# A transformer stack on one core: the last attention first, then the last two pairs' GLU one after another

## The chip, the cores and the metric

The kernel runs on one core of a Trainium2 chip. The metric is device microseconds of one execution, taken as the median over several runs. A profiled execution gives the trace, in which every instruction of every engine has its start and its length. The engines are TensorE (PE in the profile, PEld for its weight loads), VectorE (DVE), ScalarE (ACT), GpSimd (POOL) and SyncE (SP), which issues the transfers.

## The reference

The input is x, 16 sequences of 256 tokens with 128 features, in float32. Two blocks with residual follow. The first is a causal attention with 16 heads of 8 on a normalized x. The second, on the normalized sum, is a stack of 6 layers, each of them an attention in windows of 32 tokens and a gated unit (GLU):

```python
for i in range(DEPTH):                                   # 6
    x = attn_layer(shift_tokens(x), Wqkv[i], ...) + x    # 16 heads of 64, windows of 32
    x = ffn_layer(shift_tokens(x), ...) + x

def ffn_layer(x, g, bln, W1, b1, W2, b2):
    xn = layernorm(x) * g + bln
    a, gate = split(xn @ W1 + b1)                        # 341 each
    return a * gelu(gate) @ W2 + b2
```

`shift_tokens` takes half of the features from the token before. No sequence needs another one, so the stack can run over sequences and layers in a staggered order.

## The kernel before, in words

A first stage does the causal attention, writes its sum to `out` in memory and leaves the normalized, transposed sum in SBUF: `yT[b]`, 128 features by 512 tokens, that is, a pair of sequences. The second stage is the stack. It counts sequences through all layers, n = 0 to 95 (layer n // 16, sequence n % 16), and pairs m = 0 to 47; pair m is sequences 2m and 2m+1, so the last pair is 47, with n = 94 and 95, and the second last is 46.

The loop at the end runs `half(n, u)` for n from -2 to 98 and u = 0, 1. A half works on several sequences at once. For sequence n it does half of the heads: `sim` (scores, 64 matmuls per call pair), `soften` (DVE: scale `sm` and maximum `mx`; POOL: subtract), `power` (ACT: exp, tile `ex`), and, one half later, `share` (DVE: sum and reciprocal; POOL or DVE: product), `attn_T` (transposes and an ACT copy, tile `aT`) and `attn_v` (tile `po`, 64 small matmuls each for x = 0 and 1, and an ACT copy to `ao` after each). `proj_v` makes the values: matmul `v`, ACT copy `vn`, and transfers on SP from `vn` to a shifted copy `vs`. `project_out` (matmul `wo`, DVE add to `yT`) comes another half later. For later sequences the same half does `proj_qk`, norms and `shift`. Where n reaches the end, the calls for sequences that don't exist fall away (`do`), so the last halves have less and less beside them.

The GLU of a pair of 512 columns is spread over the halves of the next sequences: `glu_shift` (POOL, tile `x2`), `glu_center` (matmul `cen`, ACT square `fsq` and copy `xc`), `glu_var` (matmuls `pv`, ACT copy `vr`), `glu_turn` (transpose `vT`, DVE `var`, POOL `rstd`), `glu_norm` (transposes `rs`, DVE `xn`, POOL scale), `glu_part` three times (matmuls `hg` and `ha`, ACT gelu `g`, DVE product `h`), `glu_out` (matmuls `w`, DVE add to `yT`). Every float32 matmul stands in the trace as two passes; a pair's `hg`, `ha` and `w` are 18 passes. In the last layer `leave(s)` follows for each sequence: transposes `fin`, a load of `out[s]` into `res`, a DVE add and the store. `x2` and `g` share one buffer (tag `gl`).

In the kernel before, pair 46 is shifted in half (94, 1), centred and turned in (95, 0), normed with parts 0 and 1 in (95, 1), part 2 in (96, 0), out and left in (96, 1). Pair 47 has its shift in (96, 1) and the rest in halves of 97 and 98, which hold nothing else.

The order on each engine: `in_order` adds to each instruction of a half a dependency on the one before it on the same engine, for halves with 0 <= n < 96. So up to half (95, 1) the order on the engines is as written; after that a scheduler places the instructions.

Of the kernel before, what the change touches and what calls it, by code (L numbers as in the profile page):

```python
# [7 lines left out]
F32 = mybir.dt.float32  # L8
# [3 lines left out]
ALU = mybir.AluOpType  # L12
# [3 lines left out]
NSEQ, S, E = 16, 256, 128  # L16
# [17 lines left out]
V_G, V_B, V_B2, V_B1, V_QK = 0, 1, 2, 3, 9  # L34
# [4 lines left out]
def tile_transformer(  # L39
# [16 lines left out]
    nc = tc.nc  # L56
    P = 128
# [6 lines left out]
    ident = cst[:, C_ID : C_ID + 128]  # L64
# [6 lines left out]
    vecs = const.tile([P, DEPTH, V_ALL], F32, name="vecs")  # L71
# [17 lines left out]
    def in_order(traced, pinned):  # L89

        for i in nc.cur_bb.bb.instructions[traced:]:
            if i.engine not in engines:
                continue
            if pinned and i.engine in last:
                tc.add_manual_dep(
                    i,
                    last[i.engine],
                    mybir.DependencyInfo(mybir.DependencyClass.NoSync, mybir.DependencyReason.DATA),
                    reason="in_order",
                )  # L100
            last[i.engine] = i.name


    with ExitStack() as st:
# [249 lines left out]
        for s in range(-3, NSEQ + 3):  # L354
            traced = len(nc.cur_bb.bb.instructions)
# [22 lines left out]
    with ExitStack() as st:  # L378
# [18 lines left out]
        def psum1(name):  # L397
            return ps_o.tile([P, 512], F32, tag="o", name=name)
# [63 lines left out]
        def shifted(dst, s):  # L462
            y = yT[s // 2][:, (s % 2) * S : (s % 2 + 1) * S]
            nc.gpsimd.tensor_copy(dst[0:64, :], y[0:64, :])
            nc.gpsimd.memset(dst[64:128, 0:1], 0.0)
            nc.gpsimd.tensor_copy(dst[64:128, 1:S], y[64:128, 0 : S - 1])
# [228 lines left out]
        x2s, bcs, sms = {}, {}, {}  # L695


        def glu_shift(m):
            b = m % 8
            x2 = x2s[m] = p1.tile([P, 2 * S], F32, tag="gl", name=f"x2_{m}")  # L700
            for i in range(2):
                shifted(x2[:, i * S : (i + 1) * S], 2 * b + i)

        def glu_center(m):
            x2 = x2s.pop(m)
            ps = psum1(f"cen_{m}")
            nc.tensor.matmul(ps, center, x2, start=True, stop=True)
            sq2 = p1.tile([P, 2 * S], F32, tag="h1", name=f"fsq_{m}")
            nc.scalar.activation(sq2, ps, AF.Square)
            xc = p1.tile([P, 2 * S], F32, tag="h2", name=f"xc_{m}")  # L710
            nc.scalar.copy(xc, ps)
            xns[m] = sq2, xc

        def glu_var(m):
            sq2, xc = xns[m]
            pv = psum1(f"pv_{m}")

            for t in range(4):
                nc.tensor.matmul(
                    pv[32 * t : 32 * t + 32, :P], mean32, sq2[:, t * P : (t + 1) * P], start=True, stop=True  # L720
                )
            rows = p1.tile([P, P], F32, tag="vr", name=f"vr_{m}")
            nc.scalar.copy(rows, pv[:, :P])
            xns[m] = rows, xc

        def glu_turn(m):
            rows, xc = xns[m]
            pv = psum1(f"vT_{m}")
            nc.tensor.transpose(pv[:, :P], rows, ident)
            var = p4.tile([P, 4], F32, tag="var", name=f"var_{m}")  # L730
            nc.vector.tensor_scalar(var, pv[:, :P].rearrange("p (t k) -> p t k", k=32)[:, :, 0], 1e-5, None, ALU.add)
            rstd = p4.tile([P, 4], F32, tag="rstd", name=f"rstd_{m}")
            rsqrt(rstd, var)
            xns[m] = rstd, xc

        def glu_norm(m):
            l = m // 8
            rstd, xc = xns[m]
            ps = psum1(f"rs_{m}")
            for t in range(4):  # L740
                nc.tensor.matmul(
                    ps[:, t * P : (t + 1) * P],
                    rstd[:, t : t + 1].to_broadcast([P, P]),
                    ident,
                    start=True,
                    stop=True,
                    is_transpose=True,
                )
            xn = p1.tile([P, 2 * S], F32, tag="xn", name=f"xn_{m}")
            nc.vector.tensor_tensor(xn, ps, xc, ALU.mult)  # L750
            nc.gpsimd.tensor_scalar(xn, xn, vecs[:, l, V_G : V_G + 1], vecs[:, l, V_B : V_B + 1], ALU.mult, ALU.add)
            xns[m] = xn

        def glu_part(mm, i):
            l = mm // 8
            if mm % 8 == 0 and i == 0:
                load_glu(l)
            xn = xns[mm]
            a, m = DI_PARTS[i]
            pg, ph = psum1(f"hg_{mm}_{i}"), psum1(f"ha_{mm}_{i}")  # L760
            nc.tensor.matmul(pg[:m], W["1"][:, DI + a : DI + a + m], xn, start=True, stop=True)  # L761
            nc.tensor.matmul(ph[:m], W["1"][:, a : a + m], xn, start=True, stop=True)  # L762
            g = p1.tile([P, 2 * S], F32, tag="gl", name=f"g_{mm}_{i}")
            nc.scalar.activation(g[:m], pg[:m], AF.Gelu, bias=vecs[:m, l, V_B1 + 3 + i : V_B1 + 4 + i])
            h = p1.tile([P, 2 * S], F32, tag=f"h{i}", name=f"h_{mm}_{i}")
            nc.vector.scalar_tensor_tensor(
                h[:m], ph[:m], vecs[:m, l, V_B1 + i : V_B1 + i + 1], g[:m], ALU.add, ALU.mult
            )
            hs[mm, i] = h

        def glu_out(mm):
            l, b = divmod(mm, 8)
            ps = psum1(f"w2_{mm}")
            for i, (a, m) in enumerate(DI_PARTS):
                nc.tensor.matmul(ps, W["2"][:m, i, :], hs[mm, i][:m], start=(i == 0), stop=(i == 2))  # L775
            nc.vector.scalar_tensor_tensor(yT[b], ps, vecs[:, l, V_B2 : V_B2 + 1], yT[b], ALU.add, ALU.add)

        def leave(s):

# [17 lines left out]
        def do(n, f, *a):  # L797
            if has(n):
                f(n, *a)
# [6 lines left out]
        def half(n, u):  # L806
            even = n % 2 == 0
            m = n // 2 - 1 if even else (n - 3) // 2
            glu = lambda m: 0 <= m < N // 2
            i, j = 2 * u, 2 * u + 1  # L810
            b, bu = (n, 0) if u else (n - 1, 1)
            bi, bj = 2 * bu, 2 * bu + 1
            do(b, share, bi)
            do(b, share, bj)
            do(n, sim, u, 0)
            do(n, sim, u, 1)
            for k in range(2):
                do(n + 2, proj_qk, i, k)
            if u == 0:
                do(n + 1, sums)  # L820
            else:
                do(n + 1, spread_k, 1)
                do(n + 1, norm_k, 1)
                if not even and glu(m):
                    glu_norm(m)
            do(n, sim, u, 2)
            do(n, sim, u, 3)
            do(n, soften, i)
            do(n, soften, j)
            do(n - 1, project_out, u)  # L830
            if u:
                do(n + 3, shift)
                if even and glu(m):
                    glu_shift(m)
            elif has(n + 1):
                roots(n + 1, n2s.pop(n + 1))
            do(b, attn_T, bi)
            do(b, attn_T, bj)
            do(n, proj_v, u, 0)
            do(b, attn_v, bi)  # L840
            if not even and u == 0 and glu(m):
                glu_center(m)
            do(n + 2, proj_qk, j, 0)
            if even and u == 0 and glu(m - 1):
                glu_part(m - 1, 2)
            if not even and glu(m):
                if u == 0:
                    glu_var(m)
                else:
                    glu_part(m, 0)  # L850
                    glu_part(m, 1)
            do(n + 2, proj_qk, j, 1)
            if not even and u == 0 and glu(m):
                glu_turn(m)
            if u == 0:
                do(n + 1, spread_k, 0)
                do(n + 1, norm_k, 0)
            do(n, power, i)
            do(n, power, j)
            do(b, attn_v, bj)  # L860
            do(*((n, masks, 1) if u == 0 else (n + 1, masks, 0)))
            if even and u and glu(m - 1):
                glu_out(m - 1)
                if m - 1 >= (DEPTH - 1) * 8:
                    leave(2 * ((m - 1) % 8))
                    leave(2 * ((m - 1) % 8) + 1)
            do(n, proj_v, u, 1)

        do(0, shift)
        last.clear()  # L870
        for n in range(-2, N + 3):
            for u in range(2):
                traced = len(nc.cur_bb.bb.instructions)
                half(n, u)
                in_order(traced, 0 <= n < N)

# [94 lines left out]
```

## Time and profile before

| | us |
|---|---|
| median of 3 runs | 3625.76 (3624.58 to 3628.56) |
| the profiled execution | 3618.6 |
| its span | 3616.8 |
| PE busy in the span | 3471.4 |
| DVE / POOL / ACT busy | 2832.4 / 2570.5 / 1882.4 |

The span is the time from the first to the last event of the profile; the execution's own time is 1.8 us longer. Busy time says how long an engine had an instruction in it. The chain that ended last follows the work back from the last instruction to what released it. The granted clock is that of TensorE, 1.00 for full speed.

### The profile page before, as it was taken

How to read it: one execution, taken by the hardware profiler on the slowest of the kernel's cores; microseconds unless marked ns; L12 is line 12 of the kernel's file. 1: busy time of each engine (PE TensorE's matmuls, PEld its weight loads, DVE VectorE, ACT ScalarE, POOL GpSimd, SP SyncE). 2: the span in 40 equal slices, each digit the busy share in tenths (PEclk: the TensorE clock that was granted, in tenths of full speed). 3: DMA queues.
4: the chain of work that ended last, by engine and by line, in shares of the span. 5: the costliest groups of instructions: out<-in, count | busy, mean ns of one | idle time of the engine just before them, and what ended most of it. 6: DMA issues, size and time to landing. Idle time of an engine off the chain costs nothing.

```text
span 3616.8 us, 153872 instructions
## 1 busy us (share of the span) xinstructions
PE 3471.4 (96%) x68080; PEld 2423.2 (67%) x68080; DVE 2832.4 (78%) x4866; ACT 1882.4 (52%) x3180; POOL 2570.5 (71%) x2731
## 2 busy tenths in 40 slices
PE   7999799999999999999999999999999999999998
PEld 5777466666666666666666666666666666666664
DVE  5665788887888888888887888887887888888784
ACT  2444355555555555555555555555555555555553
POOL 3221778778777778777777777777777778777772
PEclk9999899999999999999999999999999999999999
DMA  2000333334433334343334333334433343433332
GB/s 83 8 10 10 88 98 100 101 88 111 111 100 86 97 101 109 103 106 101 80 99 119 104 91 100 96 91 117 111 95 83 100 109 90 107 104 95 100 105 61
DMA packets 249445, 331.68 MB, mean 92 GB/s; under 512 B 74446, under 2 KB 105548, under 8 KB 247884
## 3 DMA queue, kind: packets, MB, share of 16 engines
q1 hardware_dynamic: 248060, 321.14, 33.9%
q8 instruction: 536, 8.78, 1.0%
q14 instruction: 129, 1.06, 0.1%
q10 hardware_dynamic: 720, 0.70, 0.1%
HBM read 28.14 MB, written 4.19 MB: 9 GB/s over the span
## 4 chain that ended last, share of the span: by engine, by line
PE 77%; DVE 9%; issue 7%; POOL 3%; ACT 2%; DMA 2%; SPq 0%; POOLq 0%; DVEq 0%; ACTq 0%
PE qk L485 18%; PE po L668 11%; PE v L568 9%; PE wo L688 8%; PE sim L605 6%; PE w L775 4%; PE hg L761 3%; PE ha L762 3%; PE aT L648 2%; PE n L506 2%; DVE tq L558 2%; PE bc L544 2%; DVE t L487 2%; PE sim L585 2%; ACT aT L650 1%
## 5 line engine op out<-in xcount | busy, mean ns | idle before, releaser
L487 DVE TENSOR_TENSOR t<-qk,ab 128x1024 f32<-128x1024 f32 x768 | 916.1, 1218 | 280.7 <-ACT sq L486 245.1
L499 POOL TENSOR_TENSOR tq<-t 128x512 f32<-128x512 f32 x768 | 961.7, 1273 | 89.8 <-DVE t L487 66.5
L485 PE MATMUL qk<-xs,wqk 128*128 128x256 f32 x3072 | 792.1, 394 | 1.6 <-DVE yT L693 1.5
L496 POOL TENSOR_TENSOR sq<-sq 128x512 f32<-128x512 f32 x384 | 489.0, 1274 | 339.0 <-ACT sq L486 329.6
L485 PEld LDWEIGHTS qk<-xs,wqk 128*128 128x128 f32 x3072 | 555.1, 191 | 156.0 <-issue 54.9
L486 ACT ACTIVATE sq<-qk 128x512 f32<-128x512 f32 x768 | 459.4, 598 | 352.5 <-PE qk L485 345.4
L650 ACT COPY aT<-aT 128x512 f32<-128x512 f32 x384 | 207.6, 586 | 599.3 <-PE aT L648 598.8
L668 PEld LDWEIGHTS po<-aT,vs 64*64 64x64 f32 x12288 | 327.4, 134 | 203.4 <-issue 108.7
L568 PE MATMUL v<-wv,xs 128*128 128x512 f32 x768 | 421.9, 631 | 27.6 <-ACT aT L650 21.2
L626 POOL TENSOR_TENSOR sm<-sm,mx 128x512 f32<-128x512 f32 x384 | 396.2, 1043 | 29.1 <-DVE mx L625 27.8
L668 PE MATMUL po<-aT,vs 64*64 64x32 f32 x12288 | 394.3, 222 | 8.7 <-issue 4.2
L605 PEld LDWEIGHTS sim<-us 64*32 64x32 f32 x24576 | 262.0, 105 | 205.8 <-issue 190.5
L668 PE MATMUL po<-aT,vn 64*64 64x32 f32 x12288 | 386.7, 219 | 4.6 <-issue 4.6
L574 ACT COPY vn<-v 128x512 f32<-128x512 f32 x384 | 225.2, 587 | 308.3 <-PE v L568 304.9
L688 PE MATMUL wo<-ao,wout 128*128 128x256 f32 x1536 | 383.2, 392 | 1.0 <-ACT ao L677 1.0
L668 PEld LDWEIGHTS po<-aT,vn 64*64 64x64 f32 x12288 | 330.0, 135 | 6.8 <-issue 6.8
L605 PE MATMUL sim<-us 64*32 64x64 f32 (+1 forms) x24576 | 324.6, 221 | 3.5 <-DMA us<-tq 2.8
L642 POOL TENSOR_TENSOR ex<-ex,rec 128x512 f32<-128x512 f32 x288 | 296.5, 1044 | 40.4 <-DVE rec L640 19.7
L688 PEld LDWEIGHTS wo<-ao,wout 128*128 128x128 f32 x1536 | 276.0, 189 | 49.5 <-ACT ao L677 1.7
L677 ACT COPY ao<-po 128x512 f32<-128x512 f32 x384 | 222.8, 580 | 119.0 <-PE po L668 118.8
L639 DVE TENSOR_REDUCE rec<-ex 128x8 f32<-128x512 f32 x384 | 251.8, 656 | 34.1 <-ACT ex L632 34.1
L625 DVE TENSOR_REDUCE mx<-sm 128x8 f32<-128x512 f32 x384 | 263.4, 686 | 13.3
(125 smaller groups left out, 5196.4 us busy)
## 6 DMA issues: line engine op xcount, KB each, us to landing
us<-tq SPq DMA_DIRECT2D x768, 256.0 KB
vs<-vn SPq DMA_DIRECT2D x384, 192.0 KB
vs<-vn SPq DMA_DIRECT2D x192, 64.0 KB
wqk<-in_f_wqkv_dram SPq DMA_DIRECT2D x96, 64.0 KB
ab<-in_tables_dram SPq DMA_DIRECT2D x6, 1024.0 KB
wv<-in_f_wqkv_dram SPq DMA_DIRECT2D x12, 256.0 KB
wout<-in_f_wo_dram SPq DMA_DIRECT2D x24, 128.0 KB
x<-in_x_dram SPq DMA_DIRECT2D x16, 128.0 KB
```

Of the source, the lines that this page charges most:

```text
L485: nc.tensor.matmul(ps[:, t * S : t * S + S], W["qk", g][:, k, t, :], xs[n], start=True, stop=True)
L486: nc.scalar.activation(sq2[:, k].rearrange("p t n -> p (t n)"), ps, AF.Square)
L487: nc.vector.tensor_tensor(t12[:, k].rearrange("p f t n -> p f (t n)"), ps.unsqueeze(1).to_broadcast([P, 2, 2 * S]), W["ab", l][:, k].rearr ...
L496: nc.gpsimd.tensor_tensor(sq[n, g], sq2[:, :, 0, :], sq2[:, :, 1, :], ALU.add)
L499: nc.gpsimd.tensor_tensor(tq[n, g][:, t], t12[:, :, 0, t, :], t12[:, :, 1, 1 - t, :], ALU.add)
L568: nc.tensor.matmul(ps, xs[n][:, P * c : P * c + P], W["v"][:, u].rearrange("p g x d -> p (g x d)"), start=True, stop=True)
L605: nc.tensor.matmul(ps[WIN * r : WIN * r + WIN, x, col + first : col + 64], qk[part, g, 0, WIN * c : WIN * c + WIN], qk[part, g, 1, WIN * ( ...
L625: nc.vector.tensor_reduce(mx, seg, AX.X, ALU.max)
L626: nc.gpsimd.tensor_tensor(seg, seg, mx.unsqueeze(2).to_broadcast([P, 8, 64]), ALU.subtract)
L642: on.tensor_tensor(seg, seg, rec.unsqueeze(2).to_broadcast([P, 8, 64]), ALU.mult)
L668: nc.tensor.matmul(po[DH * y : DH * y + DH, h, x, g, WIN * r : WIN * r + WIN], v[64 * h : 64 * h + 64, r // 2, 2 * g + y, x, :], aT[64 * h ...
L688: nc.tensor.matmul(ps[:, :S].rearrange("p (h m) -> p h m", h=2), W["out"][:, g, 2 * u + x, :], a[:, x, :, g, :], start=(j == 0), stop=(j == 3)
```

## The change

It concerns only the end. Half (95, 1) is no longer pinned (`n < N - u`). From it on, the GLU of pair 46 does not appear in the halves any more: it stops after `glu_turn` in (95, 0). In half (96, 0), once the attention of the last sequence is through, `project_out(95, 1)` follows at once, then the rest of pair 46 (`glu_norm`, three parts, out, two `leave`), then `glu_all` for sequence 94 and for sequence 95. `glu_all` is the whole GLU of one sequence, 256 columns, with its `leave`. All the GLU functions take either a pair m or a tuple (47, 0) or (47, 1); `which` gives them the width w.

```diff
+        def which(m):
+            if isinstance(m, tuple):
+                return m[0] // 8, m[0] % 8, m[1] * S, S, f"{m[0]}_{m[1]}"
+            return m // 8, m % 8, 0, 2 * S, str(m)
...
+        def glu_all(m):
+            glu_shift(m)
+            glu_center(m)
+            glu_var(m)
+            glu_turn(m)
+            glu_norm(m)
+            for i in range(3):
+                glu_part(m, i)
+            glu_out(m)
+            leave(2 * (m[0] % 8) + m[1])
...
-            glu = lambda m: 0 <= m < N // 2
+            glu = lambda m: 0 <= m < N // 2 - 1
...
-                if not even and glu(m):
+                if not even and n < N - 1 and glu(m):
                     glu_norm(m)
...
-            do(n - 1, project_out, u)
+            if (n, u) != (N, 1):
+                do(n - 1, project_out, u)
...
-            if even and u == 0 and glu(m - 1):
+            if even and u == 0 and n < N and glu(m - 1):
                 glu_part(m - 1, 2)
-            if not even and glu(m):
+            if not even and glu(m) and (n, u) != (N - 1, 1):
                 if u == 0:
                     glu_var(m)
...
-            if even and u and glu(m - 1):
+            if even and u and n < N and glu(m - 1):
                 glu_out(m - 1)
...
             do(n, proj_v, u, 1)
+            if (n, u) == (N, 0):
+                project_out(N - 1, 1)
+                m = N // 2 - 2
+                glu_norm(m)
+                for i in range(3):
+                    glu_part(m, i)
+                glu_out(m)
+                leave(2 * (m % 8))
+                leave(2 * (m % 8) + 1)
+                glu_all((m + 1, 0))
+                glu_all((m + 1, 1))
...
-                in_order(traced, 0 <= n < N)
+                in_order(traced, 0 <= n < N - u)
```

In the built program TensorE's order at the end is: the last `po`, the first `wo` matmul, three of the four `rs` transposes of pair 46, the other `wo` and the last `rs`, `hg`, `ha` and `w` of pair 46, its four `fin`; then `cen`, `pv`, `vT`, `rs`, `hg`, `ha`, `w`, `fin` of sequence 94, and the same of sequence 95.

More of the change, by code (lines that the diff above doesn't have):

```diff
@@ L695, in tile_transformer @@
         x2s, bcs, sms = {}, {}, {}
+        def which(m):
+            if isinstance(m, tuple):
+                return m[0] // 8, m[0] % 8, m[1] * S, S, f"{m[0]}_{m[1]}"
+            return m // 8, m % 8, 0, 2 * S, str(m)
         def glu_shift(m):
[L699 to L702, printed above, removed]
+            _, b, c0, w, name = which(m)
+            x2 = x2s[m] = p1.tile([P, 2 * S], F32, tag="gl", name=f"x2_{name}")[:, :w]
+            for i in range(w // S):
+                shifted(x2[:, i * S : (i + 1) * S], 2 * b + c0 // S + i)
         def glu_center(m):
             x2 = x2s.pop(m)
-            ps = psum1(f"cen_{m}")
+            _, _, _, w, name = which(m)
+            ps = psum1(f"cen_{name}")[:, :w]
             nc.tensor.matmul(ps, center, x2, start=True, stop=True)
-            sq2 = p1.tile([P, 2 * S], F32, tag="h1", name=f"fsq_{m}")
+            sq2 = p1.tile([P, 2 * S], F32, tag="h1", name=f"fsq_{name}")[:, :w]
             nc.scalar.activation(sq2, ps, AF.Square)
-            xc = p1.tile([P, 2 * S], F32, tag="h2", name=f"xc_{m}")
+            xc = p1.tile([P, 2 * S], F32, tag="h2", name=f"xc_{name}")[:, :w]
             nc.scalar.copy(xc, ps)
@@ L715, in glu_var @@
             sq2, xc = xns[m]
-            pv = psum1(f"pv_{m}")
-            for t in range(4):
+            _, _, _, w, name = which(m)
+            nr = w // 4
+            pv = psum1(f"pv_{name}")
+            for t in range(w // P):
                 nc.tensor.matmul(
@@ L721, in glu_var @@
                 )
-            rows = p1.tile([P, P], F32, tag="vr", name=f"vr_{m}")
-            nc.scalar.copy(rows, pv[:, :P])
+            rows = p1.tile([P, P], F32, tag="vr", name=f"vr_{name}")
+            nc.scalar.copy(rows[:nr], pv[:nr, :P])
             xns[m] = rows, xc
@@ L727, in glu_turn @@
             rows, xc = xns[m]
[L728 to L732, printed above, removed]
+            _, _, _, w, name = which(m)
+            nr, nt = w // 4, w // P
+            pv = psum1(f"vT_{name}")
+            nc.tensor.transpose(pv[:, :nr], rows[:nr], ident[:nr, :nr])
+            var = p4.tile([P, 4], F32, tag="var", name=f"var_{name}")[:, :nt]
+            nc.vector.tensor_scalar(var, pv[:, :nr].rearrange("p (t k) -> p t k", k=32)[:, :, 0], 1e-5, None, ALU.add)
+            rstd = p4.tile([P, 4], F32, tag="rstd", name=f"rstd_{name}")[:, :nt]
             rsqrt(rstd, var)
@@ L736, in glu_norm @@
         def glu_norm(m):
-            l = m // 8
+            l, _, _, w, name = which(m)
             rstd, xc = xns[m]
-            ps = psum1(f"rs_{m}")
-            for t in range(4):
+            ps = psum1(f"rs_{name}")[:, :w]
+            for t in range(w // P):
                 nc.tensor.matmul(
@@ L748, in glu_norm @@
                 )
-            xn = p1.tile([P, 2 * S], F32, tag="xn", name=f"xn_{m}")
+            xn = p1.tile([P, 2 * S], F32, tag="xn", name=f"xn_{name}")[:, :w]
             nc.vector.tensor_tensor(xn, ps, xc, ALU.mult)
@@ L754, in glu_part @@
         def glu_part(mm, i):
-            l = mm // 8
-            if mm % 8 == 0 and i == 0:
+            l, b, _, w, name = which(mm)
+            if b == 0 and i == 0:
                 load_glu(l)
@@ L759, in glu_part @@
             a, m = DI_PARTS[i]
-            pg, ph = psum1(f"hg_{mm}_{i}"), psum1(f"ha_{mm}_{i}")
+            pg, ph = psum1(f"hg_{name}_{i}")[:, :w], psum1(f"ha_{name}_{i}")[:, :w]
             nc.tensor.matmul(pg[:m], W["1"][:, DI + a : DI + a + m], xn, start=True, stop=True)
             nc.tensor.matmul(ph[:m], W["1"][:, a : a + m], xn, start=True, stop=True)
-            g = p1.tile([P, 2 * S], F32, tag="gl", name=f"g_{mm}_{i}")
+            g = p1.tile([P, 2 * S], F32, tag="gl", name=f"g_{name}_{i}")[:, :w]
             nc.scalar.activation(g[:m], pg[:m], AF.Gelu, bias=vecs[:m, l, V_B1 + 3 + i : V_B1 + 4 + i])
-            h = p1.tile([P, 2 * S], F32, tag=f"h{i}", name=f"h_{mm}_{i}")
+            h = p1.tile([P, 2 * S], F32, tag=f"h{i}", name=f"h_{name}_{i}")[:, :w]
             nc.vector.scalar_tensor_tensor(
@@ L771, in glu_out @@
         def glu_out(mm):
-            l, b = divmod(mm, 8)
-            ps = psum1(f"w2_{mm}")
+            l, b, c0, w, name = which(mm)
+            ps = psum1(f"w2_{name}")[:, :w]
             for i, (a, m) in enumerate(DI_PARTS):
                 nc.tensor.matmul(ps, W["2"][:m, i, :], hs[mm, i][:m], start=(i == 0), stop=(i == 2))
-            nc.vector.scalar_tensor_tensor(yT[b], ps, vecs[:, l, V_B2 : V_B2 + 1], yT[b], ALU.add, ALU.add)
+            y = yT[b][:, c0 : c0 + w]
+            nc.vector.scalar_tensor_tensor(y, ps, vecs[:, l, V_B2 : V_B2 + 1], y, ALU.add, ALU.add)
+        def glu_all(m):
[8 more added lines that the diff above has]
+            leave(2 * (m[0] % 8) + m[1])
         def leave(s):
```

## The prediction

> **What bounds the kernel now.** I read the page first, then the chain that ended last, then the end of the trace in order of time, then the granted clock. The page says that TensorE carries the kernel:
>
> ```profile
> span 3616.8 us, 153872 instructions
> PE 3471.4 (96%) x68080; PEld 2423.2 (67%) x68080; DVE 2832.4 (78%) x4866; ACT 1882.4 (52%) x3180; POOL 2570.5 (71%) x2731
> ```
>
> That holds until about 3580 us. The order of instructions of the changed program differs from the old one, apart from line numbers, only from the second half of sequence 95 on (v_0_1, at 3565.44). So the question is the last 50 us alone, where no later sequence fills TensorE. Pieces of the chain there (start, length, engine, tile, line, count):
>
> ```profile
> 3591.28 1.73 PE w L775 x4
> ...
> 3593.84 0.66 PE fin L783 x4
> 3594.50 0.87 PE cen L707 x2
> ...
> 3597.53 1.01 POOL rstd L84
> ...
> 3601.00 2.07 PE hg L761 x2
> ...
> 3609.10 2.59 PE w L775 x6
> ...
> 3611.78 0.76 DVE yT L776
> ```
>
> The last output projection (wo) ends at 3591.28. From there to the start of cen (3594.50) only 3.22 us go to the rest of pair 46: its GLU is by then mostly done beside the attention. Then pair 47 runs alone: a front of small steps passed between engines (cen 3594.50 to hg 3601.00, 6.50 us), the 18 passes of hg, ha and w (3601.00 to 3611.78, 10.78 us) and the way out (5.02 us). The clock over the same time (stretch, its length, busy us of PE, PEld, DVE, ACT and POOL, then the granted clock):
>
> ```profile
> 3592.79:3596.21 3.42, 1.89 (x15) 0.85 (x14) 1.51 (x3) 0.82 (x2) 0.00 (x0) 1.00 0.13 38
> 3596.21:3599.62 3.41, 1.24 (x13) 0.55 (x5) 0.40 (x2) 0.52 (x2) 1.01 (x1) 1.00 0.40 116
> 3599.62:3603.03 3.41, 2.03 (x3) 1.00 (x4) 0.45 (x1) 0.00 (x0) 0.77 (x1) 0.50 0.00 0
> 3603.03:3606.45 3.42, 3.42 (x6) 1.35 (x5) 0.75 (x1) 0.69 (x1) 0.00 (x0) 0.50 0.00 0
> 3606.45:3609.86 3.41, 3.41 (x10) 1.35 (x9) 1.40 (x2) 1.37 (x2) 0.00 (x0) 1.00 0.00 0
> ```
>
> All of the trace's changes of clock that I looked up fall on one grid of 3.41 us. The stretch of the front, 36% busy, is followed by half clock; the stretch of 59% did not lift it, the one of 100% did. Earlier, 1.80 of 3.41 us (53%) also led to half clock at 3545.00, while 55% (3592.79) did not. So 5.43 us of the 18 passes (3601.00 to 3606.43) ran at half speed and cost 2.72 us; at full clock they would take 8.06.
>
> **Part 1, attention first.** From (95, second half) on, glu_norm, glu_part and glu_out of pair 46 leave the attention, and with them two exchanges of the activation table (1.28 us each). The half is no longer pinned, so the reductions come as both sm, then both mx. Step by step: v_0_1 ends at 3566.56; 128 sim matmuls in a row took 1.39 us (3555.03), so sim ends at 3568.0 instead of 3568.99, no rs between. DVE: two sm and the first mx, at 0.66 us each and 0.69, to 3570.1. POOL subtracts (1.04), to 3571.25 and 3572.3. ACT stands behind two aT copies (to 3571.7), then ex_2 (0.57), vn (0.59), ex_3 (0.57), ao (0.59): 3574.0. The second half of po waits for that ao copy, as it did at 3587.36, and ends at 3575.1; its ao at 3575.85; six passes of wo (1.30) to 3577.2; the aT transposes (0.55) to 3577.75; aT copy to 3578.1; po (1.06) 3579.2; ao 3579.95; po 3581.06; ao 3581.8; wo 3583.15. The last projection is thus 8.1 us earlier than 3591.28. The new exchange of the table (1.28) runs from 3581.8 and lies beside wo; without that cover it would cost up to 1.28.
>
> **Part 2, pair 46 exposed.** What ran beside the attention is now behind it. On DVE the last yT add (0.42), then xn (0.69), on POOL the scale (0.77), with hand-offs 2.1 us: hg at 3585.25. 18 passes of 512 columns at full clock: 8.06. yT add and four fin, as 3593.04 to 3594.50 with the hand-off: 1.46. Then cen can start at 3594.77. So the 8.1 us are given back here: +0.27 against 3594.50. The load and store of res on SP stay behind the same instructions as before and have 10 us of room.
>
> **Part 3, pair 47 by sequence.** Both halves go through the whole chain, and in TensorE's order cen of sequence 95 stands behind fin of sequence 94: nothing of one covers the other. The shift also needs the buffer gl, free after the last h; its 0.97 us on POOL fit beside w and fin. Behind this wait on POOL stand only rstd and the scale of the same sequence, which need it anyway. Price of 256 columns from rows of narrower tiles:
>
> ```profile
> L693 DVE TENSOR_TENSOR yT<-wo,yT 128x256 f32<-128x256 f32 x192 | 79.3, 413 | 4.4 <-PE wo L688 4.4
> L511 ACT COPY n<-n 128x256 f32<-128x256 f32 x96 | 35.8, 373 | 41.8 <-PE n L506 41.8
> L84 POOL TENSOR_TENSOR rstd_a<-var_a,cst 128x2 f32<-128x2 f32 x16 | 11.5, 719 | 85.4 <-DVE var_a L171 85.4
> L176 POOL TENSOR_SCALAR xn_a<-x,mv_a,rstd_a 128x128 f32<-128x128 f32 x32 | 25.2, 795 | 1.6
> ```
>
> Front, against 6.50: cen -0.41 (0.21 a pass fewer, as in the wo rows), square and variance -0.30, rstd -0.31 (1.02 to 0.72), rs -0.24 (two transposes fewer), xn -0.27 (0.69 to 0.42), scale -0.27: 4.70. The scale has no row: between the 0.39 of a 64x256 copy and the 0.795 of L176; I take 0.50, near the copy, since 512 columns take 0.77. The 18 passes, 3.85 us at full clock, are then bound by gelu and product handing one buffer to and fro: gelu between 0.37 (L511) and 0.69, I take 0.47; product between 0.41 and 0.75, I take 0.48; 1.07 a round, 4.55 in all. Between the sequences (yT, two fin) 0.98. The way out with one res instead of two and a half yT: 4.30. The upper ends of these prices add 0.3 to each front and up to 1.4 to each 4.55; at half clock the latter disappear behind TensorE.
>
> At full clock throughout: 3594.77 + 4.70 + 4.55 + 0.98 + 4.70 + 4.55 + 4.30 = 3618.55, or +1.75.
>
> **Part 4, the clock.** It decides the size. Three pauses come, each with about 30 to 47% busy in some stretch of 3.41 us. Before pair 46's hg the pause is 1.9 us after a busy time with gaps: a stretch under 53% for about 6 in 10 places of the grid; one stretch at half clock then costs 1.71. Before each of the two last hg there are nearly 6 us with under 2 us of work: a stretch below 53% whatever the place. Half clock then lasts 3.0 to 6.4 us into the passes (until the end of the first full stretch), and the passes take 4.1 plus half of that, 5.6 to 7.3, that is +1.05 to +2.75 over 4.55 for each sequence, +1.9 in the middle. Sum: 1.75 + 1.71 + 3.80 = +7.26: span 3624.1, execution 3625.9 against 3618.6. The old kernel's 5.43 us of half clock are 0.7 above the middle of the same 3.0 to 6.4, so against its median it is 0.36 more: 3625.76 + 7.6 = 3633.4.
>
> The Trainium skill, "TensorE: Matmul & The Clock Gate", Part 1, has TensorE fall to half clock after an idle window of about 3.4 us and rise after a busy one. In the strict reading of idle no pause here is long enough, and the sum would be the +1.75. The rows above (36% busy, then 0.50) speak against that reading.
>
> **Rivals.** (1) The pause before pair 46 stays above 53% and only the last two chains meet half clock: +5.9. For it: 1.9 us is short. Against: the po steps before it have gaps too. (2) Further waits in the new last half, whose gaps no row shows. The vs transfer of the last v is issued about 3574.65 and needed at 3578.6; at the 5.71 us of the one at 3538.26 it comes 1.8 late. Half clock in po and wo: po took 1.93 instead of 1.06 at 3545.63, which for two po and a wo is about 3.0. One or both on top of +7.3 to +9.3: +9 to +14. For it: the new half waits at nearly every step. Against: the vs transfers after 3567 found quiet queues. (3) Clock full throughout: +1.75. (4) Faster: sequence 94's front has all its inputs while attention of 95 still runs. If the front overlapped what is ahead of it, each 4.70 would be covered and TensorE kept busy: 1.75 - 2 x 4.70 - 0.98 = -8.6, 3617.1. It decides at TensorE's queue: cen would have to run before pair 46's hg. The order of instructions puts it after, and in the trace of before matmuls start in the order of the program.
>
> **How the numbers follow.** A measurement of this kernel can tell about 0.2%, 7.25 us, from no change. The forecast (three chains at half clock, +5.9 to +9.3) has 0.46, some six tenths of it above 7.25; rival 1 (+4.2 to +7.6) 0.18, a tenth above; rival 2 0.26, all above; rival 3 0.04, rival 4 0.06. Slower: 0.28 + 0.02 + 0.26 = 0.56; same: 0.18 + 0.16 + 0.04 = 0.38; faster 0.06. The range leaves out rivals 3 and 4 and the far end of rival 2, and takes the lower ends of the phases and the price bounds: +2.2 to +12.2, 3628 to 3638.
>
> **What would show it.** Last wo near 3583 and cen of sequence 94 near 3595 to 3597: parts 1 and 2 right. cen to hg near 4.7 twice, and granted clock 0.50 at both last hg: parts 3 and 4 right. It is wrong if the second cen starts before the first sequence's w ends, if the clock stays at 1.00, or if wo ends after 3586.

## The result, and the profile after

| | before | after |
|---|---|---|
| median, us (22 runs each) | 3621.43 (3614.84 to 3630.58) | 3629.19 (3620.86 to 3635.26) |
| span of the profiled execution, us | 3616.8 | 3633.5 |
| tail, us | 64.02 | 70.47 |

The ratio is 1.0022, 95% interval 1.0015 to 1.0028: slower by 8.0 us (5.4 to 10.1). The interval holds the 7.25 us (0.2%) that the prediction took as the least that a measurement can tell and doesn't reach zero. The 22 runs of before have a median 4.3 us below the three that the prediction started from.

The two spans differ by 16.7 us, but most of that isn't the change. The first `yT` add of layer 0 is 6.3 us later in the one execution than in the other (558.6 and 564.9), and the yT add of pair 45, near the end of what both programs do in the same order, 10.25 us later (3552.78 and 3563.03). So all profiles are compared by their **tail**: from the start of pair 45's yT add to the end of the span. From that add to the first matmul v of sequence 95's second half, where the orders part, every profile below takes the same 12.65 or 12.66 us. There the change costs 70.47 - 64.02 = 6.45 us.

The page, for the span and TensorE (PE):

```profile
span 3633.5 us, 153939 instructions
PE 3482.8 (96%) x68101; PEld 2433.8 (67%) x68101; DVE 2834.5 (78%) x4872; ACT 1880.0 (52%) x3184; POOL 2571.4 (71%) x2733
```

TensorE has 21 instructions more and is busy 11.4 us longer, of which 2.86 us lie in the tail (53.75 against 50.89). The chain that ended last in the changed kernel, in order of time (start, length, engine, tile, line, count):

```profile
3592.47 1.32 PE wo L688 x6
...
3595.76 1.12 PE hg L772 x2
...
3603.80 0.76 DVE yT L788
...
3605.26 0.45 PE cen L714 x2
...
3607.56 0.70 POOL rstd L84
...
3610.01 1.22 PE hg L772 x2
...
3617.32 0.50 DVE yT L788
...
3618.30 0.45 PE cen L714 x2
...
3623.06 1.22 PE hg L772 x2
...
3629.24 0.49 DVE yT L788
```

Note the same front of small steps twice, cen to hg: 3605.26 to 3610.01 and 3618.30 to 3623.06, with the whole of the first sequence's passes between. The granted clock over these stretches of the changed kernel (columns as in the prediction):

```profile
3592.33:3595.75 3.42, 1.56 (x9) 1.08 (x7) 1.02 (x2) 1.13 (x1) 0.77 (x1) 1.00 0.00 0
...
3605.99:3609.40 3.41, 1.12 (x7) 0.47 (x7) 0.58 (x2) 0.65 (x3) 0.69 (x1) 1.00 0.47 137
3609.40:3612.81 3.41, 2.80 (x7) 2.26 (x8) 0.48 (x1) 0.47 (x1) 0.55 (x1) 0.50 0.06 17
3612.81:3616.23 3.42, 3.42 (x10) 2.42 (x9) 0.96 (x2) 0.94 (x2) 0.08 (x1) 0.50 0.00 0
3619.64:3623.05 3.41, 0.70 (x3) 0.33 (x3) 0.58 (x2) 0.26 (x1) 1.26 (x2) 1.00 0.13 38
3623.05:3626.47 3.42, 3.41 (x8) 2.78 (x9) 0.48 (x1) 0.91 (x2) 0.00 (x0) 0.50 0.02 5
```

Stretches 33% and 21% busy (1.12 and 0.70 of 3.41 us) are followed by half clock; the first sequence's passes meet two stretches of it, the second's one. The pause before pair 46 (first line, 46%) is not followed by it.

### The profile page after: what moved, and what is told of

Same layout as the page of the kernel before. It is cut to its first block, busy times and chain, and to the rows that moved or that the text cites. A ratio compares the mean times of both kernels' runs of the same rounds, so it can differ in the third digit from the quotient of the medians.

```text
span 3633.5 us, 153939 instructions
## 1 busy us (share of the span) xinstructions
PE 3482.8 (96%) x68101; PEld 2433.8 (67%) x68101; DVE 2834.5 (78%) x4872; ACT 1880.0 (52%) x3184; POOL 2571.4 (71%) x2733
## 4 chain that ended last, share of the span: by engine, by line
PE 78%; DVE 8%; issue 7%; POOL 3%; ACT 2%; DMA 2%; SPq 0%; POOLq 0%; DVEq 0%; ACTq 0%
PE qk L485 18%; PE po L668 11%; PE v L568 10%; PE wo L688 8%; PE sim L605 7%; PE w L786 4%; PE hg L772 3%; PE ha L773 3%; PE aT L648 3%; PE n L506 2%; DVE tq L558 2%; PE bc L544 2%; DVE t L487 2%; PE sim L585 2%; ACT aT L650 1%
## 5 line engine op out<-in xcount | busy, mean ns | idle before, releaser
L642 POOL TENSOR_TENSOR ex<-ex,rec 128x512 f32<-128x512 f32 x288 | 296.9, 1045 | 38.1 <-ACT vn L574 16.7
```

What stands on the lines that cost most here:

```text
L642: on.tensor_tensor(seg, seg, rec.unsqueeze(2).to_broadcast([P, 8, 64]), ALU.mult)
```

## The experiments

All of them change only the end of the program, and each was timed beside the kernel before. Tails are from one profile each, ratios from all runs.

**e1_pair** keeps attention-first and pair 46 behind it, but runs pair 47 as one pair:

```diff
-            leave(2 * (m[0] % 8) + m[1])
+            leave(2 * (m % 8))
+            leave(2 * (m % 8) + 1)
...
-                glu_all((m + 1, 0))
-                glu_all((m + 1, 1))
+                glu_all(m + 1)
```

> Attention first and pair 46 after it as in the changed kernel, but pair 47 as one pair of 512 columns. Measured by the tail, from the yT add of pair 45 to the end of the span: 64.0 us before, 70.5 after. Theory (the loss is the split by sequence: a second front, a second way out, a second stretch of half clock): cen near 42.2 us into the tail as in the changed kernel, front 6.5, 18 passes 8.1 plus 1.5 to 3.2 for half clock, way out 5.0, so a tail of 63.3 to 65.0, about that of before. Rival (the loss is pair 46 behind the attention): the tail stays at 69 to 71.

Measured: 3618.43 us, ratio 1.0001 (0.9991 to 1.0011), tail 65.15. The chain of e1_pair:

```profile
3594.84 2.59 PE w L786 x6
...
3598.92 0.87 PE cen L714 x2
...
3605.43 2.08 PE hg L772 x2
...
3615.06 0.76 DVE yT L788
```

Without the split the time is that of before. Here the pause before pair 46 did lead to half clock:

```profile
3584.65:3588.06 3.41, 1.53 (x8) 1.05 (x7) 1.02 (x2) 0.78 (x1) 0.77 (x1) 1.00 0.00 0
3588.06:3591.48 3.42, 3.42 (x5) 1.35 (x4) 0.14 (x1) 0.69 (x1) 0.00 (x0) 0.50 0.00 0
```

Pair 46's passes took 9.73 us instead of 8.04: the 1.69 that put the tail 0.15 over the expected range.

**e2_split** is the other part alone: attention, its pinning and pair 46 as before, and pair 47 by sequence.

```diff
-                if not even and n < N - 1 and glu(m):
+                if not even and glu(m):
...
-            if (n, u) == (N, 0):
...
+            if (n, u) == (N, 1):
...
                 m = N // 2 - 2
...
                 glu_all((m + 1, 0))
                 glu_all((m + 1, 1))
...
-                in_order(traced, 0 <= n < N - u)
+                in_order(traced, 0 <= n < N)
```

> The split alone: pair 46 and the attention as before, in the pinned order, only pair 47 by sequence. Theory: cen starts 41.7 us into the tail as before, then 4.75 + 5.6 to 7.3 + 0.98 + 4.75 + 5.6 to 7.3 + 4.3, a tail of 67.7 to 71.1, slower than before by 4 to 7 us. Rival (pair 46 behind the attention is the loss): 64 to 65, as before.

Measured: 3631.48 us (5 runs), ratio 1.0036 (1.0024 to 1.0048), tail 71.07. The fronts are 4.75 us each, the passes 7.32 and 6.20, nearly the figures of the changed kernel. So the split carries the loss. How large it is by time isn't settled: 13.0 us (8.7 to 17.4) from five runs is more than the 4 to 7 expected and more than the 7.05 of the tail, and the cause of that is open. The interval of the ratio meets that of the whole change. In the profile cen comes 1.1 us later in the tail than before (42.83 against 41.72), behind a stretch of half clock that the profile of before doesn't have there:

```profile
3571.07:3574.48 3.41, 2.34 (x83) 1.63 (x83) 1.46 (x4) 2.78 (x6) 1.25 (x2) 1.00 0.22 58
3574.48:3577.90 3.42, 3.42 (x69) 1.75 (x69) 1.26 (x3) 0.78 (x2) 0.79 (x1) 0.50 0.03 5
```

**e3_fill** keeps the whole change and puts bfloat16 matmuls into the pauses, whose result nobody reads:

```diff
         def glu_all(m):
             glu_shift(m)
             glu_center(m)
+            fill(2)
             glu_var(m)
+            fill(1)
             glu_turn(m)
+            fill(4)
             glu_norm(m)
+            fill(4)
             for i in range(3):
                 glu_part(m, i)
             glu_out(m)
+            fill(1)
```

(and `fill(6)` and `fill(2)` around pair 46, with TensorE's order pinned from there).

> The changed kernel with bf16 matmuls of 512 columns in TensorE's pauses of the three last fronts, on data that nobody reads, and TensorE pinned from there on. Theory (half clock is the larger part of what the split costs): granted clock 1.00 at both last hg, their passes 4.5 to 4.8 each instead of 7.3 and 6.2, the fronts unchanged within 0.4 each, a tail of 65.5 to 67, that is 3.5 to 5 less than the changed kernel. Rival (the passes are bound by gelu and product, the clock does not matter): passes and tail as in the changed kernel.

Measured: 3621.44 us, ratio 1.0012 (1.0001 to 1.0023), tail 66.69. The windows of e3_fill over its two fronts:

```profile
3600.70:3605.46 4.76, 4.14 (x22) 1.47 (x20) 1.16 (x4) 0.91 (x3) 1.25 (x2) 1.00 0.38 110
3611.25:3616.02 4.77, 4.14 (x22) 1.47 (x20) 1.01 (x3) 0.91 (x3) 1.26 (x2) 1.00 0.11 31
```

TensorE is 87% busy in each front (4.14 of 4.76), the clock stays at 1.00 through the tail, and the passes fall from 7.31 and 6.18 to 4.81 and 4.81: 3.87 us of the 6.45. The fronts keep their length, so the fillers delay nothing there. Of the tail's excess over before 2.67 us remain. The times alone would not settle this, as the intervals of 1.0012 and 1.0022 overlap.

**e4_front94** gives the last sequences buffers of their own and writes the front of sequence 94 ahead of the last `project_out`:

```diff
-                project_out(N - 1, 1)
                 m = N // 2 - 2
+                glu_front((m + 1, 0))
+                project_out(N - 1, 1)
                 glu_norm(m)
...
-                glu_all((m + 1, 0))
-                glu_all((m + 1, 1))
+                glu_back((m + 1, 0))
+                glu_front((m + 1, 1))
+                glu_back((m + 1, 1))
```

> The changed kernel with the front of sequence 94 (shift to scale, in buffers of its own) ahead of the last output projection instead of behind pair 46; nothing else is moved by hand. Theory (fronts are latency, which TensorE's order exposes): the front of 94 takes 4.75 + 0.45 from the tail, its passes follow pair 46's at full clock (4.0 to 4.6 instead of 7.3), the last projection comes about 1 us later, since rs of 94 stands before it and waits for rstd: tail 70.5 - 5.2 - 2.9 + 1 = 63.4, 62 to 65. Rival (TensorE is full there and the front costs as much beside the attention): 68 to 71.

Measured: 3619.71 us, ratio 1.0006 (0.9996 to 1.0017), tail 64.83. The chain of e4_front94 around sequence 94's passes:

```profile
3597.86 0.43 PE hg L782 x2
...
3601.96 0.49 DVE yT L798
...
3602.93 0.45 PE cen L721 x2
...
3607.90 1.22 PE hg L782 x2
```

Sequence 94 now follows pair 46 at once, at full clock, and takes 4.10 us; with buffers of their own gelu and product no longer bound its passes. One front is gone from the end and, with the half clock that followed it, 5.6 us of the tail. By time it is 2.2 us (-1.4 to +6.2) above before, which meets the interval of the change. It isn't free: hg of pair 46 starts 34.49 us into the tail instead of 32.73, since the rs transposes stand in TensorE's queue ahead of the last wo and wait for rstd.

**e6_unpin** is the kernel before with only the pin taken from the last half of sequence 95:

```diff
-                in_order(traced, 0 <= n < N)
+                in_order(traced, 0 <= n < N - u)
```

> The kernel before, with only the second half of sequence 95 no longer pinned: one part of the change alone. TensorE's order stays the same; on ScalarE the exps ex_2 and ex_3 come ahead of the gelus of pair 46's parts 0 and 1, which takes out two table loads of 1.28 us; on VectorE the reductions of the last half change places with the products h. My theory: in the kernel before, aT, ao and po behind those table loads waited 1.4 to 2.4 us each, so the last wo comes 3 to 5 us earlier and the tail is 59 to 61 us, ratio 0.9985 to 0.9993. Then a part of what attention-first gains in the change comes from the order on ScalarE and not from moving pair 46. Rival: TensorE's order binds (the wo ahead of aT waits for the same po as before), the tail stays at 64 plus or minus 1, ratio 0.9995 to 1.0005.

Measured: 3620.41 us, ratio 1.0001 (0.9991 to 1.0012), tail 61.02. ScalarE of e6_unpin in order of time:

```profile
3575.28 0.65 ACT L632 ACTIVATE ex<-sm 128x512 f32<-128x512 f32 x1
3575.81 0.60 ACT L677 COPY ao<-po 128x512 f32<-128x512 f32 x1
3576.43 1.28 ACT L764 ACT_TABLE_LOAD   x1
```

Both exps are done before the first gelu's table load, and two loads are gone. The last wo ends 35.76 us into the tail instead of 38.50, and what follows is as before, half clock included. So of the 7.74 us by which the change brings the last wo forward (30.76), 2.74 come from the order alone. Both figures lie just outside the expectation (3 to 5 us for the last wo, a tail of 59 to 61). The trace says 3 us for the whole; the interval of the times (-3.3 to +4.3 us) holds both that and nothing.

**e5_all** writes the last half out by hand, with TensorE pinned: the front of sequence 94 beside the attention, that of 95 among pair 46's passes, buffers of their own for both.

```diff
+            project_out(n, 0)
+            attn_v(n, 3)
+            glu_turn(a)               # a, c: sequences 94 and 95
+            glu_part(m, 0)            # m: pair 46
+            project_out(n, 1)
+            glu_norm(a)
+            glu_shift(c)
+            glu_part(m, 1)
+            glu_center(c)
+            glu_part(m, 2)
+            glu_var(c)
+            glu_turn(c)
+            glu_out(m)
+            glu_norm(c)
...
+            glu_part(c, 1)
+            leave(2 * (a[0] % 8))
+            glu_part(c, 2)
```

> The new order of the end with the split by sequence kept, but with the fronts of sequences 94 and 95 written beside the attention and among pair 46's passes, with buffers of their own, and TensorE's order there pinned by hand. My theory: the split itself costs nothing once each front has other passes of TensorE beside it, and the half clock goes with the pauses. Then the tail (yT add of pair 45 to the end of the span; 64.0 in the kernel before, 70.5 in the changed one) falls to 53 to 57 us, no stretch after the last wo falls below 50% busy ahead of a last hg, and the three groups of passes take 8.1, 4.1 to 4.8 and 4.1 to 4.8 at full clock. Time 7 to 11 us below the kernel before, ratio 0.997 to 0.998. Rival: VectorE, ScalarE and GpSimd, which must now serve the attention and a front at once, become the bound, and the last wo comes later by what the fronts take: tail 60 to 65 and a ratio of 0.999 to 1.000.

Measured: 3614.75 us, ratio 0.9984 (0.9974 to 0.9994), tail 55.00, the clock full until the matmuls end. The last wo is 2.6 us later than in the changed kernel (33.33 against 30.76, and 38.50 before), less than the fronts take, and the rival's tail of 60 to 65 did not come. The gain by time is 5.8 us (2.2 to 9.4), where 7 to 11 were expected; by the tail it is 9.0. The trace showed a wait that could go: the last product h stood behind the residual add of sequence 94, which waited for its load until 3610.93.

**e8_best** puts that `leave` one step later:

```diff
-            leave(2 * (a[0] % 8))
             glu_part(c, 2)
+            leave(2 * (a[0] % 8))
```

> e5_all with the leave of sequence 94 one step later, behind the last product h. In e5_all the last h stood on VectorE behind the residual add of sequence 94, which waited for its load until 3610.93, and TensorE's last w waited 0.48 us. Theory: the last h comes 0.7 us earlier, tail 54.3 (53.5 to 55), all else as in e5_all; a difference that only the trace can show, and the time is again 5 to 10 us under the kernel before. Rival: the last yT add now stands behind that residual add and nothing is won, tail 55.0 to 55.5.

Measured: 3609.95 us, ratio 0.9973 (0.9962 to 0.9984), tail 54.10. Its interval meets that of e5_all; the 0.9 us between the two are the trace's alone. The chain of e8_best after the last wo:

```profile
3589.25 1.73 PE wo L688 x8
3590.97 0.22 PE rs L762 x2
...
3596.03 2.77 PE w L796 x6
3598.81 0.22 PE rs L762 x2
3599.03 0.43 PE hg L782 x2
...
3606.30 1.31 PE w L796 x6
...
3607.64 0.49 DVE yT L798
```

From the last wo to the end of the last w TensorE is busy for 16.27 of 16.64 us, and no front stands there as a stretch of its own.

**e7_pairend** has the same order, but pair 47 as one pair, its front among pair 46's passes:

```diff
+            project_out(n, 1)
+            glu_shift(a, 1)           # a: pair 47, its second sequence
+            glu_part(m, 1)
+            glu_center(a)
+            glu_part(m, 2)
+            glu_var(a)
+            glu_turn(a)
+            glu_out(m)
+            glu_norm(a)
...
+            for i in range(3):
+                glu_part(a, i)
+            glu_out(a)
```

> The order of e5_all with its pinning and own buffers, but pair 47 as one pair of 512 columns again: its front stands among pair 46's passes, after the last output projection. It asks whether the split by sequence brings anything once the fronts are covered. My theory: no. The front of a pair (6.5 us alone) is covered by pair 46's passes except for about 1 us; its 18 passes take 8.1 at full clock and the way out 5.0. From the last wo (33.3 into the tail in e5_all) that makes 22 to 23 us, tail 55 to 57 us, within 2 us of e5_all's 55.0, and no half clock. Rival: the split does bring something when covered, since it lets the second sequence's passes cover the first one's way out and halves the front that hangs on the last projection; then this kernel's tail is 58 to 62.

Measured: 3612.16 us, ratio 0.9974 (0.9963 to 0.9985), tail 56.64. In time it can't be told from e8_best; in the trace it is 2.5 us behind, of which TensorE's wait for the scale of xn ahead of the last hg is 0.81. So the split adds at most these 2.5 us. What wins is the order that the last three kernels share. It holds several things at once (the exps ahead of the gelus, pair 46's norm ahead of the last wo, the covered front, no half clock, buffers of their own), and the runs don't price each of them alone.

## Why the prediction was right, point by point

The direction, the cause and the size held: 3629.19 lies in the range, and the change costs 8.0 us against the 7.6 of the sum, the tail 6.45 against 7.26. How near the sums came is in part luck. At full clock the change costs 2.58 (6.45 - 3.87) where the sum had 1.75, and the 1.71 taken for pair 46, which did not come in the profile, hides that. And 3633.4, the time forecast, is 4.2 above the measured one because its starting point was 4.3 above the median of 22 runs; the range was wide enough for that. By its steps:

- **Part 1** (last wo 8.1 us earlier): 7.74. The order of the exps did what the steps said; e6_unpin shows that without moving pair 46 it would have been 2.74.
- **Part 2** (cen +0.27): +0.51, with pair 46's passes at 8.04 against 8.06. Attention first gives back what it wins, and e1_pair shows it with the time.
- **Part 3**: fronts 4.75 and 4.76 against 4.70, between the sequences 0.98 against 0.98, way out 4.26 against 4.30. The passes at full clock were mis-sized by 0.26 each (4.81 in e3_fill against 4.55). The scale, the one price without a row, took 0.56 against the 0.50 taken.
- **Part 4**: half clock came at both last hg. It cost 7.31 + 6.18 - 2 x 4.81 = 3.87, against 3.80 predicted as +1.9 each. The **1.71 for pair 46** did not come in the profiled execution, whose pause was 46% busy, under the 53% taken as the bound. It came in e1_pair, whose program is the same up to there, after a stretch 45% busy. The sum counted the term in full; what the runs show is a term that comes in one profile and not in the other, and the bound of 53% is no rule.

The terms of the tail, measured: +0.51 (to cen), +3.01 (fronts, 9.51 against 6.50), +2.71 (passes, 13.49 against 10.78), +0.98 (between), -0.76 (way out): +6.45.

Of the rivals, the profiled execution itself is rival 1 (+5.9 forecast, +6.45 measured). e1_pair went as the forecast there, and the median over 22 runs can't part the two. Rival 2 fell: no vs transfer stands in the chain of the changed kernel's last half, the clock was 1.00 in its po and wo, and the last wo came 0.4 us later than the sum. Rival 3 is what e3_fill makes of the change: +2.67 of tail against +1.75. Rival 4 did not happen, for the reason given (cen behind pair 46's fin in TensorE's order), but its price was near: written in another order, the end of e8_best is 9.9 us shorter than before by the tail, against the 8.6 worked out. Two differences cancel in this: the last wo of e8_best is 2.8 us later than in the sum (33.17 into the tail against 30.37), and what follows it 4.1 shorter (20.9 against 25.0).

The Trainium skill, "TensorE: Matmul & The Clock Gate", Part 1, puts the fall of the clock down to an idle window of about 3.4 us. Here it fell after stretches of 3.41 us that were 21% and 33% busy, so the strict reading of idle did not hold, while the length of the stretch agrees. Keeping TensorE busy, which e3_fill did with matmuls of no use, kept the clock at 1.00.

## What to carry to other kernels

At the end of this program a chain of small steps costs its whole length, and again the half clock that its pause brings on for the work behind it. Cutting the last tile in two brings both twice, each time a little smaller (fronts of 9.51 us together against 6.50, half clock of 3.87 against 2.72), unless each part's chain is written beside other work of TensorE. Look first for the order of instructions that covers it, with buffers that allow it, before asking how the work is cut: here the new order, which covers the fronts, won about 10 us, some 3 of them by the order of the exps alone (e6_unpin, by its trace), and with it the pair and the split could not be told apart in time. Compare two profiles from the last point at which the programs are still the same, since the executions may have drifted apart by more than the change is worth.

## What the runs showed of the hardware that was not expected

- A stretch 46% busy (1.56 of 3.42 us, changed kernel) left the clock at 1.00, while one of 45% with the same work (1.53 of 3.41, e1_pair), one of 53% (1.80 of 3.41, before) and one of 69% (2.34 of 3.41, e2_split) were followed by 0.50. The share of TensorE's modelled busy time in a stretch doesn't decide by itself; what else does is open.
- The same program is up to some 20 us apart between runs, and the granted clock goes with it: in the 11 runs of e4_front94, 3615.80 us at a mean clock of 0.992 and 3633.67 at 0.987. The missing 0.005 of the clock, taken as lost time, is an estimated 18 us (0.005 x 3620), and the times differ by 17.9. So part of the spread of this kernel looks like stretches at half clock that fall differently; this was not tested by a run, and it isn't the whole: in e8_best two runs at the same mean clock of 0.991 took 3603.66 and 3618.71 us.
